# A four-layer graph network on one core: attention of layer 2 in 32-column groups, row sums on GpSimd and ScalarE, layer 0 with its values stationary

## The chip, the cores and the metric

The kernel runs on one core of a Trainium2 chip. The metric is device time in microseconds, the median over runs: 3777.71 us of three runs (3777.58 to 3783.42) for the kernel before.

A core has five engines, each working through its own queue in order. TensorE (PE) multiplies matrices and writes to PSUM, a memory of eight banks of 128 x 512 fp32. VectorE (DVE) and ScalarE (ACT) do elementwise work and read PSUM as well as SBUF, the working memory of 128 partitions; ScalarE also evaluates functions such as exp and ln. GpSimd (POOL) does elementwise work in SBUF. SyncE (SP) issues most DMAs. They wait for each other by semaphores.

## What is computed

32 graphs of 512 nodes with 256 features pass through four layers, each followed by a sum with its input and a layernorm. The layers 0, 1 and 3 are graph attention whose weights come from one value per row and one per column; layer 2 is a transformer block with eight heads of 32 and a mask.

```python
# layer 0: 4 heads of 64; node_adj is 0 or 1 here
h = jnp.einsum('bnd,hde->bhne', nodes_embed, W)
weight = mask * (e_src[:, :, t, :, None] + e_dst[:, :, t, None, :])
weight = jnp.where(node_adj[:, None] == 0, NEG, leaky_relu(weight, 0.01))
dst = jnp.einsum('bhij,bhje->bhie', softmax(weight, axis=-1), h) + bias
out = relu(dst) + h                      # then a layernorm over each head's 64
...
# layer 2: 8 heads of 32
scores = jnp.einsum('bhqd,bhkd->bhqk', q * scale, k)
scores = jnp.where(allowed[:, None], scores, -jnp.inf)   # adj or its transpose or the diagonal
ctx = jnp.einsum('bhqk,bhkd->bhqd', jax.nn.softmax(scores, axis=-1), v)
attn_out = ctx @ Wo.T + bo
x = layernorm(x + attn_out); ff = relu(x @ W1.T + b1) @ W2.T + b2
```

All data are fp32.

## The kernel before

A graph's 512 nodes are four blocks of 128 (R = 4), its 256 features two (K = 2). `graph(b)` is a generator that records one graph's work in small units; each `yield` hands back a place, a number from the table `PLACES` plus `PERIOD` times the graph's number. `heapq.merge` runs the units of all 32 graphs in the order of their places, so that stages of three or four graphs lie beside each other. TensorE's instructions stand in exactly this order (`manual_schedule`); those of the other engines are put in order by a scheduler when the program is built. TensorE works through its queue without overtaking, so a product whose input is late holds everything behind it.

Buffers come from pools. A tile of a tag takes one of its `bufs` buffers and waits until the earlier tile there is no longer used. Each stage has its set ("a": masks and layers 0 and 1; "b": Q/K/V, attention, projection; "c": feed forward, layer 3). PSUM is split alike: `bank` gives two banks to "a", four to "b", two to "c". `part` gives 512-column SBUF tiles: 7, 6 and 5. Every TensorE instruction of the profile has the line L106, since the helper `product` records them all, so they are told apart by the names of their tiles.

Layer 0 (`layer0`): `project` gives h and one source and one destination value per head. The softmax needs no row maximum: with f(s + d) split into exponentials, a row's weights are max(exp(-0.99 s), exp(0.99 d)) times the edge, up to a factor of the row. `along` transposes a head's source values into a row that is equal on all partitions (`gp` in PSUM, `gb` in SBUF); `kept` (L399, VectorE) makes the four weight tiles `pt` of a head (keys on partitions, 512 queries along the row). Then `pt` is the stationary operand, 128 queries at a time, and the values `hv` of the head stream through, 64 columns and a 65th that gives the row's sum: four query blocks by four key blocks, 16 products a head. A reciprocal (L434) and a product (L435) on VectorE end the head in the row layout of `y`. Layer 1 (`o1`) and layer 3 (`o3`) do the same with 257 columns in `attend`.

Layer 2: `qkv` makes Q and K transposed, splits each into a high and a low part and spreads them by 64 KB DMAs on SyncE into the tiles `qk` (three buffers of a pair of heads), so that one product of 128 rows gives an fp32 score. `attention` goes through pairs of heads: four score units (a pair of 512-column scores `s`, exp on ScalarE L559, product with the mask on VectorE L562 or, in the last block, a further product with `shut` on TensorE), then eight products `cp` with V as the stationary operand: 64 columns per head, of which 32 are values and the 33rd is a column of ones that gives the sums. The two heads lie in columns 0 to 63 and 64 to 127 of the array. ScalarE copies `cp` to `cs` (L578). `attended` turns `cs` back into rows (16 transposes `ctp`), divides there (L593, L597), transposes again (8 more `ctp`) and multiplies with Wo (`wop`, L618). Feed forward is 16 units of eight records (`f1p`, relu L644, `f2p`).

Of the kernel before, what the change touches and what calls it, by code (L numbers as in the profile page):

```python
# [26 lines left out]
PERIOD = 12054  # L27
PLACES = {
    "edges": [-2144, -1150, -1132, 1169],
    "x": [2625],  # L30
    "mask": [15570, 16616, 16754, 17543],
    "layer 0": [
        279, 2912, 3852, 3852, 4592, 5702, 5702, 5712, 5965, 5965, 6558, 6558, 6558, 6558,
        6558, 7681, 7681, 7681, 8072, 8072, 8418, 8418, 8418, 8521,
    ],
    "layer 1": [10979, 10979, 11459, 11543, 11663, 11665, 11925, 13128, 13554, 14195, 14884],
    "qkv": [16746, 17776, 18212, 18212, 18212, 18900, 18900, 19096, 20269, 21288],
    "attention": [
        12293, 21738, 21738, 22018, 22018, 22292, 22292, 22687, 22687, 23019, 23479, 23677,
        23718, 23726, 23726, 23726, 25094, 25250, 25378, 25960,  # L40
    ],
    "projection": [26272, 26272, 26332, 26382, 27451, 27561, 28792, 29200, 29412, 29811],
    "feed forward": [
        30548, 31062, 31829, 32245, 32245, 32541, 32692, 33753, 33965, 34306, 34732, 34800,
        35052, 35117, 35751, 36541, 37158, 37317,
    ],
    "layer 3": [39718, 39718, 40714, 40734, 40817, 41334, 41569, 42319, 42319, 42339, 42339],
# [3 lines left out]

# [22 lines left out]
def fast_path(ctx: ExitStack, tc: tile.TileContext, a: dict, out: bass.AP, bad: bass.AP):  # L74
# [21 lines left out]
    VC = DH + 1  # L96
    ND = R * (H + 2 + H2)
    NL = 6
    NV = R * (NL + H)
# [13 lines left out]
    def paced(b, name, units):  # L113

        i = 0
        while True:
            stage[0] = STAGES.get(name, "b")
            try:
                next(units)
            except StopIteration as end:  # L120
                return end.value
            yield PERIOD * b + PLACES[name][i]
            i += 1
# [18 lines left out]
    v = const.tile([P, R, H2 * VC + 2 * DH - VC], F32, name="v")  # L142
    nc.gpsimd.memset(v, 1.0)
# [110 lines left out]
    def bank(name, dtype=F32):  # L254
        shape = [P, 2048 // (2 if dtype == BF16 else 4)]
        n = 4 if stage[0] == "b" else 2
        return ps.tile(shape, dtype, tag="mm" + stage[0], name=name, bufs=n)

    def part(name):

        return buf([P, N], "part", name, {"a": 7, "b": 6, "c": 5}[stage[0]])
# [80 lines left out]
    def along(cols, name):  # L342
# [7 lines left out]
        g = buf([P, N], "gb", name, {"a": 2}.get(stage[0], 1))  # L350
# [52 lines left out]
    def layer0(x, xt, at, rd, mv, var):  # L403
# [12 lines left out]
        nc.vector.tensor_mul(values, values, hv[:, :, :, HO:].to_broadcast([P, R, H, HO]))  # L416
        y = sb.tile([P, R, D], F32, tag="y", name="y0", bufs=3)
        for hh in range(H):
            gb = yield from along(ex[:, 0, hh, :].unsqueeze(2), "gb0")
            pt = [kept("pt0", gb, at[:, j, :], ex[:, 1, hh, j : j + 1]) for j in range(R)]  # L420
            p = bank("o0")
            o = p[:, : R * HC].rearrange("p (r c) -> p r c", r=R)
            for r in range(R):
                yield
                for j in range(R):
                    product(nc.tensor.matmul,
                    o[:, r, :],
                        pt[j][:, r * P : (r + 1) * P],
                        hv[:, j, hh, :],
                        start=j == 0,  # L430
                        stop=j == R - 1,
                    )
            rdh = rd[:, hh * R : (hh + 1) * R].unsqueeze(2)
            nc.vector.reciprocal(rdh, o[:, :, HO:])  # L434
            nc.vector.scalar_tensor_tensor(  # L435
                y[:, :, hh * HO : (hh + 1) * HO],
                o[:, :, :HO],
                0.0,
                rdh.to_broadcast([P, R, HO]),
                op0=ALU.max,  # L440
                op1=ALU.mult,
            )
# [48 lines left out]
    def qkv(x):  # L491
        xt = yield from transposed([x[:, r, :] for r in range(R)], "xt2")
        qk = []
        for c in range(K):
            t = [sb.tile([P, 2, 2, N], F32R, tag="qk", name="qk", bufs=3) for _ in range(2)]
            for s in range(2):
# [18 lines left out]
                for hh in range(4):  # L515
                    for g in range(4):
                        src = (hi, lo)[(g >> s) & 1]
                        nc.sync.dma_start(
                            t[hh // 2][g * DH : (g + 1) * DH, s, hh % 2, :].bitcast(F32),
                            src[hh * DH : (hh + 1) * DH].bitcast(F32),  # L520
                        )
            qk += t
        for r in range(R):
            yield
            p = bank("vp")
            for k in range(K):
# [7 lines left out]
            nc.scalar.copy(  # L534
                v[:, r, : H2 * VC].rearrange("p (h e) -> p h e", h=H2)[:, :, :DH],
                p[:, :D].rearrange("p (h e) -> p h e", h=H2),
            )
# [3 lines left out]
    def attention(qk, a2, shut):  # L541
        cs = []
        for hp in range(H2 // 2):
            pr = []
            for j in range(R):
                yield
                t = sb.tile([P, 2, N], F32, tag="pr", name="pr", bufs=4)
                for i in range(2):
                    s = bank("s")
                    product(nc.tensor.matmul,  # L550
                    s,
                        qk[hp][:, 1, i, j * P : (j + 1) * P],
                        qk[hp][:, 0, i, :],
                        start=True,
                        stop=j < R - 1,
                    )
                    if j == R - 1:
                        product(nc.tensor.matmul, s, identb, shut, start=False, stop=True)
                    nc.scalar.activation(t[:, i, :], s, AF.Exp, scale=QSCALE)  # L559
                if j < R - 1:  # L560
                    edges = a2[:, j, :].unsqueeze(1).to_broadcast([P, 2, N])
                    nc.vector.tensor_mul(t, t, edges)  # L562
                pr.append(t)

            yield
            cp = bank("cp")
            for j in range(R):
                for i in range(2):
                    first = (2 * hp + i) * VC
                    product(nc.tensor.matmul,  # L570
                    cp[i * 2 * DH : (i + 1) * 2 * DH, :],
                        v[:, j, first : first + 2 * DH],
                        pr[j][:, i, :],
                        start=j == 0,
                        stop=j == R - 1,
                    )
            t = part("cs")
            nc.scalar.copy(t, cp)  # L578
            cs.append(t)
        return cs  # L580

    def attended(x, cs, rd):
        ctx_ = []
        for r in range(R):
            yield
            p = bank("ctp")
            for hp in range(H2 // 2):
                product(nc.tensor.transpose,
                    p[:, hp * P : (hp + 1) * P], cs[hp][:, r * P : (r + 1) * P], ident
                )  # L590
            o = p.rearrange("p (h e) -> p h e", h=H2)
            rdr = rd[:, r * H2 : (r + 1) * H2].unsqueeze(2)
            nc.vector.reciprocal(rdr, o[:, :, DH : DH + 1])  # L593
            if r % 2 == 0:
                t = part("ctx").rearrange("p (r d) -> p r d", d=D)
            ctx_.append(t[:, r % 2, :])
            nc.vector.tensor_mul(  # L597
# [816 lines left out]
```

## Time and profile before

| | |
|---|---|
| median of three runs | 3777.71 us |
| the profiled execution: its own time | 3783.98 us |
| the profiled execution: span | 3782.1 us |
| TensorE busy | 3695.1 us |
| VectorE busy | 2659.2 us |
| ScalarE busy | 2034.2 us |
| GpSimd busy | 6.2 us |
| granted TensorE clock, mean | 0.982 |

The span goes from the first to the last instruction of one profiled execution; all durations below come from it. "Busy" is the time in which an engine has at least one instruction in work. The costliest groups of instructions by tile (columns: line, engine, operation, output<-input, shapes, count | busy us, mean ns of one | idle us just before them and what ended it):

```profile
L559 ACT ACTIVATE pr<-s 128x512 f32<-128x512 f32 x1024 | 557.2, 604 | 171.6 <-PE s L106 171.5
...
L106 PE MATMUL o<-hv,pt 128*128 128x65 f32 x4096 | 510.7, 279 | 10.4 <-DVE pt L399 10.4
L106 PE MATMUL f2p<-wf,ft 128*128 128x256 f32 x2048 | 490.2, 382 | 6.4 <-ACT ft L644 6.3
...
L106 PE MATMUL cp<-pr,v 128*64 128x512 f32 x2048 | 469.8, 600 | 0.0
...
L106 PE MATMUL s<-qk 128*128 128x512 f32 x1024 | 412.0, 493 | 4.8 <-ACT pr L559 4.8
```

The second number of a MATMUL row is a modelled duration with the pipeline's length in it: 16 records of 600 ns do not take 9.6 us. What a row costs on TensorE is read from the start of one row to the start of the next.

### The profile page before, as it was taken

To read this page: it belongs to the slowest core of one execution; us is meant where nothing else is said; L and a number is where in the kernel's file an instruction comes from. 1 tells how busy PE (TensorE), PEld (TensorE's weight loads), DVE (VectorE), ACT (ScalarE), POOL (GpSimd) and SP (SyncE) were. 2 spreads that over 40 slices of the span, in tenths; PEclk is the share of its full clock that TensorE was granted. 3 is DMA by queue.
4 is the path that set the end of the run, shared out by engine and by line. 5 is a ranking of instruction groups with operands and counts; after the bars stand their busy time and mean duration, and the time that the engine had idled before them with its cause. 6 is when DMAs were issued, how large, how long until landed. Compare 5 with 4: busy or idle time off the path is not lost.

```text
span 3782.1 us, 53679 instructions
## 1 busy us (share of the span) xinstructions
PE 3695.1 (98%) x19238; PEld 2832.8 (75%) x19238; DVE 2659.2 (70%) x5434; ACT 2034.2 (54%) x4705; POOL 6.2 (0%) x43
## 2 busy tenths in 40 slices
PE   5899999999999999999999999999999999999996
PEld 4577777777777777777787777777777778777765
DVE  4667776777776677776677677677677678677653
ACT  2445565555556555556555565555565555565552
POOL 0000000000000000000000000000000000000000
PEclk6899999999999999999999999999999999999998
DMA  3322222232222222222222222222222222222220
GB/s 105 83 76 59 70 65 71 73 84 61 70 64 71 76 79 63 70 65 72 73 78 65 69 66 70 73 79 68 73 62 68 73 79 68 72 63 61 56 56 12
DMA packets 180434, 261.23 MB, mean 69 GB/s; under 512 B 36801, under 2 KB 72769, under 8 KB 180161
## 3 DMA queue, kind: packets, MB, share of 16 engines
q1 hardware_dynamic: 180160, 257.71, 24.6%
q8 instruction: 156, 2.56, 0.3%
q14 instruction: 118, 0.96, 0.1%
HBM read 106.57 MB, written 16.78 MB: 33 GB/s over the span
## 4 chain that ended last, share of the span: by engine, by line
PE 95%; DVE 3%; ACT 1%; issue 0%; DMA 0%; SPq 0%; ACTq 0%; DVEq 0%
PE o L106 24%; PE cp L106 12%; PE f2p L106 12%; PE f1p L106 12%; PE s L106 8%; PE qkp L106 6%; PE h1p L106 3%; PE h3p L106 3%; PE vp L106 3%; PE h0p L106 3%; PE wop L106 3%; PE gp L106 2%; PE ctp L106 2%; PE xt1p L106 1%; PE xt3p L106 1%; PE ytp L106 1%
## 5 line engine op out<-in xcount | busy, mean ns | idle before, releaser
L562 DVE TENSOR_TENSOR pr<-pr,a 128x1024 f32<-128x1024 f32 x384 | 462.2, 1217 | 357.2 <-ACT pr L559 357.0
L559 ACT ACTIVATE pr<-s 128x512 f32<-128x512 f32 x1024 | 557.2, 604 | 171.6 <-PE s L106 171.5
L399 DVE SCALAR_TENSOR_TENSOR pt<-gb,ex,at 128x512 f32<-128x512 f32 x768 | 527.0, 745 | 36.8 <-ACT gb L351 36.8
L106 PEld LDWEIGHTS o<-hv,pt 128*128 128x128 f32 x4096 | 510.9, 199 | 23.8 <-DVE pt L399 8.3
L106 PE MATMUL o<-hv,pt 128*128 128x65 f32 x4096 | 510.7, 279 | 10.4 <-DVE pt L399 10.4
L106 PE MATMUL f2p<-wf,ft 128*128 128x256 f32 x2048 | 490.2, 382 | 6.4 <-ACT ft L644 6.3
L106 PE MATMUL o<-h,pt 128*128 128x257 f32 x2048 | 485.4, 384 | 6.5 <-DVE pt L399 6.2
L106 PE MATMUL f1p<-yt,wf 128*128 128x256 f32 x2048 | 487.2, 380 | 0.3 <-DVE yt L308 0.3
L106 PE MATMUL cp<-pr,v 128*64 128x512 f32 x2048 | 469.8, 600 | 0.0
L644 ACT ACTIVATE ft<-f1p,cols 128x256 f32<-128x256 f32 x512 | 217.8, 472 | 468.4 <-PE f1p L106 468.3
L106 PEld LDWEIGHTS o<-h,pt 128*128 128x128 f32 x2048 | 384.5, 191 | 102.7 <-PE cp L106 24.3
L106 PEld LDWEIGHTS f2p<-wf,ft 128*128 128x128 f32 x2048 | 376.2, 190 | 82.9 <-issue 26.0
L106 PEld LDWEIGHTS f1p<-yt,wf 128*128 128x128 f32 x2048 | 383.7, 190 | 55.6 <-DVE yt L308 0.7
L106 PE MATMUL s<-qk 128*128 128x512 f32 x1024 | 412.0, 493 | 4.8 <-ACT pr L559 4.8
L282 ACT ACTIVATE y<-y,rs 128x256 f32<-128x256 f32 x768 | 398.3, 591 | 28.4 <-DVE rs L278 28.4
L106 PEld LDWEIGHTS cp<-pr,v 128*64 128x64 f32 x2048 | 135.8, 137 | 257.1 <-issue 159.6
L275 DVE BATCH_NORM_STATS2 bn<-y 128x6 f32<-128x256 f32 x768 | 293.7, 410 | 3.7
L434 DVE RECIPROCAL rd<-o 128x4 f32<-128x4 f32 x128 | 23.3, 182 | 341.6 <-PE o L106 341.6
L106 PEld LDWEIGHTS s<-qk 128*128 128x128 f32 x1024 | 192.9, 191 | 59.9 <-issue 26.8
L106 PE MATMUL qkp<-xt,wqkv 128*128 128x512 f32 x512 | 231.3, 594 | 0.1
L351 ACT COPY gb<-gp 128x512 f32<-128x512 f32 x192 | 112.9, 588 | 151.9 <-PE gp L106 151.9
L578 ACT COPY cs<-cp 128x512 f32<-128x512 f32 x128 | 75.0, 586 | 188.0 <-PE cp L106 187.8
(137 smaller groups left out, 4498.5 us busy)
## 6 DMA issues: line engine op xcount, KB each, us to landing
qk<-hi SPq DMA_DIRECT2D x1024, 64.0 KB, 2.0
qk<-lo SPq DMA_DIRECT2D x1024, 64.0 KB, 2.0
adjt<-in_adjt SPq DMA_DIRECT2D x64, 512.0 KB, 3.9
adj<-in_adj SPq DMA_DIRECT2D x64, 512.0 KB, 3.2
xt<-in_xt SPq DMA_DIRECT2D x32, 512.0 KB, 3.3
x<-in_x SPq DMA_DIRECT2D x32, 512.0 KB, 4.8
out<-y SPq DMA_DIRECT2D x32, 512.0 KB, 3.1
wf<-in_w1t SPq DMA_DIRECT2D x1, 1024.0 KB, 8.6
```

The lines of the kernel that those rows point to most:

```text
L106: latest[0] = what(*args, **kwargs).ins.name
L275: nc.vector.bn_stats(st[:, r, :], y[:, r, :])
L282: nc.scalar.activation(y[:, r, :], y[:, r, :], AF.Identity, bias=rs[:, 1, r : r + 1], scale=rs[:, 0, r : r + 1],)
L351: nc.scalar.copy(g, p)
L399: nc.vector.scalar_tensor_tensor(t, g, f, edges, op0=ALU.max, op1=ALU.mult)
L434: nc.vector.reciprocal(rdh, o[:, :, HO:])
L559: nc.scalar.activation(t[:, i, :], s, AF.Exp, scale=QSCALE)
L562: nc.vector.tensor_mul(t, t, edges)
L578: nc.scalar.copy(t, cp)
L644: nc.scalar.activation(ft[:, f, :], p[:, f, :], AF.Relu, bias=bf1[:, ff + f : ff + f + 1])
```

## The change

Seven edits:

1. Layer 0: the values `hv` are now the stationary operand and `pt` streams through. All four `gb` rows are made first; then, for each key block j, four `pt` tiles, four products of 64 columns into two banks `o0` (two heads a bank) and four of 32 columns into a bank `den0` (the last of them the sums). The three banks are copied to SBUF (`back`), transposed (12 transposes `backp`), and divided there.
2. Layer 2, `attention`: four heads at a time (c = 0, 1), their two score pairs alternating; after every second key block a burst of 16 `cp` records, with V as 32 columns per head, so that four heads lie side by side in the array. No column of ones.
3. The sums of layer 2: GpSimd adds the `pr` tiles of the four key blocks (`add_to`, six adds of 128 x 1024 for each c); four products with a 32-column tile of ones (`den`) add over partitions and give the sum in all 32 rows of a head; ScalarE copies it, takes Ln and Exp(-x), and VectorE multiplies `ct` with it. The second call of `divide` is the last unit of attention. `cp` is copied straight into `ct`, so that `attended` begins at Wo: its 24 transposes and its divisions are gone.
4. Q/K spreading: the columns of the Q and K weights are paired (`wqkvp`), and one DMA of 128 KB carries two heads.
5. PSUM: one set of eight banks for all stages.
6. SBUF: `part` has 9 tiles in "a" and 6 in "c", and holds `gb` too; `pr` has 7 buffers of 128 x 1024 instead of 4.
7. `PLACES` has new numbers; the period is unchanged.

```diff
-    "attention": [
-        12293, 21738, 21738, 22018, 22018, 22292, 22292, 22687, 22687, 23019, 23479, 23677,
...
+    "attention": [
+        18973, 20977, 22864, 22903, 23000, 23000, 23000, 23000, 23117, 23194, 23655, 24186,
...
-        n = 4 if stage[0] == "b" else 2
-        return ps.tile(shape, dtype, tag="mm" + stage[0], name=name, bufs=n)
+        return ps.tile(shape, dtype, tag="mm", name=name, bufs=8)
 
     def part(name):
-        return buf([P, N], "part", name, {"a": 7, "b": 6, "c": 5}[stage[0]])
+        return buf([P, N], "part", name, {"a": 9, "c": 6}[stage[0]])
...
-        g = buf([P, N], "gb", name, {"a": 2}.get(stage[0], 1))
+        g = part(name)
...
+        gbs = []
+        for hh in range(H):
+            gbs.append((yield from along(ex[:, 0, hh, :].unsqueeze(2), "gb0")))
+        den, *ops = (bank(name) for name in ("den0", "o0", "o0"))
+        for j in range(R):
+            pt = [kept("pt0", gbs[hh], at[:, j, :], ex[:, 1, hh, j : j + 1]) for hh in range(H)]
+            yield
+            for hh in range(H):
+                product(nc.tensor.matmul,
+                    ops[hh // 2][hh % 2 * HO : (hh % 2 + 1) * HO, :],
+                    hv[:, j, hh, :HO],
+                    pt[hh],
...
+            for hh in range(H):
+                product(nc.tensor.matmul,
+                    den[hh * DH : (hh + 1) * DH, :],
+                    hv[:, j, hh, HC - DH :],
+                    pt[hh],
...
+        for i, o in enumerate((den, *ops)):
+            t = part("back")
+            evacuate(i, t, o)
+            back.append(t)
...
+        for i in range(1 + H // 2):
+            yield
+            p = bank("backp")
             for r in range(R):
...
+                product(nc.tensor.transpose,
+                    p[:, r * P : (r + 1) * P], back[i][:, r * P : (r + 1) * P], ident
+                )
...
-                for hh in range(4):
+                for hp in range(2):
                     for g in range(4):
                         src = (hi, lo)[(g >> s) & 1]
                         nc.sync.dma_start(
-                            t[hh // 2][g * DH : (g + 1) * DH, s, hh % 2, :].bitcast(F32),
-                            src[hh * DH : (hh + 1) * DH].bitcast(F32),
+                            t[hp][g * DH : (g + 1) * DH, s].bitcast(F32),
+                            src[hp * 2 * DH : (hp + 1) * 2 * DH].bitcast(F32),
                         )
...
+        def add_halves(pr):
+            for hp in range(2):
+                add_to(pr[0][hp], pr[2][hp])
+
+        def divide(c, sums):
+            den = bank("den")
+            for hh in range(4):
+                product(nc.tensor.matmul,
+                    den[hh * DH : (hh + 1) * DH, :],
+                    ones,
+                    sums[hh // 2][:, hh % 2, :],
...
+            t = buf([P, N], "dens", "dens", 2)
+            nc.scalar.activation(t, den, AF.Copy, accum_out=spread[:, 2 * c : 2 * c + 1])
+            nc.scalar.activation(t, t, AF.Ln)
+            nc.scalar.activation(
+                t, t, AF.Exp, scale=-1.0, accum_out=spread[:, 2 * c + 1 : 2 * c + 2]
+            )
+            nc.vector.tensor_mul(ct[:, c, :], ct[:, c, :], t)
+
+        for c in range(K):
+            cp = bank("cp")
+            last, pr = pr, []
             for j in range(R):
+                pr.append([])
+                for hp in range(2):
+                    yield
+                    if last and (j, hp) == (1, 0):
+                        add_halves(last)
+                    t = sb.tile([P, 2, N], F32, tag="pr", name="pr", bufs=7)
...
+                for jj in (j - 1, j):
+                    for hh in range(4):
+                        product(nc.tensor.matmul,
+                        cp[hh * DH : (hh + 1) * DH, :],
+                            v[:, jj, (4 * c + hh) * DH : (4 * c + hh + 1) * DH],
+                            pr[jj][hh // 2][:, hh % 2, :],
...
+                for hp in range(2):
+                    add_to(pr[j - 1][hp], pr[j][hp])
+                if last and j == 1:
+                    yield
+                    divide(0, last[0])
+            nc.scalar.copy(ct[:, c, :], cp)
+        yield
+        add_halves(pr)
+        yield
+        divide(1, pr[0])
+        return ct
+
+    def add_to(t, u):
+        nc.gpsimd.tensor_add(t, t, u)
```

## The prediction

> **What bounds the kernel now.** I read three views in this order: the page's busy times and chain of waits, the busy times of a stretch of ten graphs, and the TensorE timeline of one graph.
>
> ```profile
> span 3782.1 us, 53679 instructions
> ...
> PE 3695.1 (98%) x19238; PEld 2832.8 (75%) x19238; DVE 2659.2 (70%) x5434; ACT 2034.2 (54%) x4705; POOL 6.2 (0%) x43
> ...
> PE 95%; DVE 3%; ACT 1%; issue 0%; DMA 0%; SPq 0%; ACTq 0%; DVEq 0%
> ```
>
> ```profile
> 1000.00:2131.00 1131.00, 1131.00 (x6002) 872.61 (x6001) 825.46 (x1691) 633.99 (x1472) 1.05 (x10) 1.00 0.25 71
> ```
>
> The second fence is a window of 1131 us (columns: length, then busy time of PE, PEld, DVE, ACT, POOL). TensorE has no gap in it. The timeline gives the period: the transposes `xt1p` of neighbouring graphs start at 1861.66 and 1974.76 us, 113.1 us apart. 32 periods are 3619 us; 163 us of the span are start and end, where one graph alone can't fill TensorE. So a graph costs what TensorE's own queue costs; VectorE needs 825.46 / 10 = 82.5 us of the 113.1, ScalarE 63.4, GpSimd 0.1.
>
> A busy row overlaps the next one, so I take TensorE's prices from start to next start:
>
> ```profile
> 1860.70 1.03 PE L106 MATMUL cp<-pr,v 128*64 128x512 f32 x4
> 1861.66 1.09 PE L106 MATMUL xt1p<-ident,y 128*128 128x128 f32 x8
> ```
>
> ```profile
> 1958.16 3.65 PE L106 MATMUL cp<-pr,v 128*64 128x512 f32 x16
> 1961.75 1.99 PE L106 MATMUL f2p<-wf,ft 128*128 128x256 f32 x8
> ...
> 1974.76 1.09 PE L106 MATMUL xt1p<-ident,y 128*128 128x128 f32 x8
> ...
> 2005.67 1.91 PE L106 MATMUL ctp<-ident,cs 128*128 128x128 f32 x16
> 2007.41 1.06 PE L106 MATMUL h0p<-w,xt 128*128 128x264 f32 x4
> ...
> 2030.60 5.31 PE L106 MATMUL qkp<-xt,wqkv 128*128 128x512 f32 x12
> 2035.75 3.64 PE L106 MATMUL o<-h,pt 128*128 128x257 f32 x16
> 2039.22 0.60 PE L106 MATMUL ytp<-ident,y 128*128 128x128 f32 x4
> 2039.66 3.68 PE L106 MATMUL o<-hv,pt 128*128 128x65 f32 x32
> 2043.18 0.60 PE L106 MATMUL gp<-ident,ex 128*128 128x128 f32 x4
> ```
>
> Twelve `qkp` records take 5.15 us, 0.429 us for 512 columns. (A product of fp32 is two records.) Sixteen `cp` records of the same 512 columns take 3.59 us, not 6.9: each uses 64 output columns, and two run at once. 8 x 0.429 = 3.43; with the slower first record behind the burst I count 0.34 us for entering and leaving this mode, 3.77 a burst. A transpose costs 1.74 / 16 = 0.109. The 32 records of one head of layer 0 take 3.52 us, 0.110 each, although 65 columns would stream in far less: each loads 128 columns of weights.
>
> **What the skill says.** The Trainium skill, "TensorEngine Tiling (Array Packing)", Tiling Modes, has 128x64 as two tiles and 128x32 as four, each running its own loads and matmuls, and a drain at a change of mode. The trace agrees for two (3.59 us) and shows the drain (0.34); it has no four. "SBUF — State Buffer", Who interferes with whom: a VectorE instruction with two SBUF inputs and a GpSimd instruction that reads SBUF share one port, and the later one is blocked for the whole of the earlier. No run here shows it yet. "GPSIMD Engine Reference", Elementwise, gives 4497 ns for an fp32 add of 2048 elements.
>
> **The change, for one graph, on TensorE.**
> - Gone: layer 0's four heads, 4 x 3.52 = 14.1. Gone: four `cp` bursts, 4 x 3.77 = 15.1. Gone: 16 + 8 transposes `ctp`, 2.6. Sum 31.8.
> - Layer 0 new: per block j, eight records for the values (64 columns, two at once: 4 x 0.429 = 1.72), eight for the sums (32 columns, four at once: 0.86), the mode's edges 0.34 and half as much for the change of width: 3.08, four times 12.3.
> - `cp` new: the same 64 records, four at once, in four bursts of 16: 4 x 0.429 + 0.34 = 2.06, together 8.2. `den`: twice 0.86, one right behind a `cp` burst, one alone (0.34): 2.1. `backp`: 12 x 0.109 = 1.3.
> - Net 31.8 - 23.9 = 7.9 us less; a gapless period would be 105.2. Scores, feed forward, layers 1 and 3 and projections keep their counts. Bound of the unknown: if four groups run no faster than two, `cp` gains nothing (+6.9), `den` +1.7 and `den0` +3.4, so 12 us more. I take four at once, because two cost nothing extra.
>
> **VectorE, ScalarE, SyncE.** VectorE loses L434 and L435 (23.3 + 54.3 = 77.6 us over 32 graphs, 2.4), L593 and L597 (2.1), one `ct` copy (0.7), and gains two reciprocals (0.4), two products out of PSUM, one copy and two `ct` products (five of about 0.68, the `y<-f2p` row): 1.4 less, 81 of 105. ScalarE loses four `cs` copies and a `ct` copy (2.9) and gains two `ct` copies, two `back` copies and twice copy, Ln, Exp with two accumulator reads (2.2 each): +3.8, so 67. Both lie beside TensorE; if TensorE's cover went, VectorE would be next. The Q/K spreading becomes 1024 DMAs of 128 KB for 2048 of 64 KB (2.0 us to landing). The fourth Q/K tile now waits for both head pairs' walk through all keys, since pairs alternate. From its release to its first use TensorE has some 14 us of work (four feed-forward units of 1.7, a `cp` burst, `xt1p`, scores), against 2 us and some issuing; the graph's output and the next loads queue behind it on SyncE, all needed later. I cost it at nothing.
>
> **GpSimd and the waits, which decide.** Twelve adds of 128x1024 per graph are new. The trace has only a write:
>
> ```profile
> L141 POOL MEMSET hv<- 128x1040 f32 x1 | 1.0, 969 | 0.0
> ...
> L399 DVE SCALAR_TENSOR_TENSOR pt<-gb,ex,at 128x512 f32<-128x512 f32 x768 | 527.0, 745 | 36.8 <-ACT gb L351 36.8
> ...
> L562 DVE TENSOR_TENSOR pr<-pr,a 128x1024 f32<-128x1024 f32 x384 | 462.2, 1217 | 357.2 <-ACT pr L559 357.0
> ```
>
> An add can't take less than that write, 1.0 us; the skill's figure gives an estimate of 2.25; with each add waiting for a VectorE instruction to finish (1.2) and stretching, 3.4. I take 2.25: 27 us of GpSimd per graph. Of VectorE's work some two thirds have two SBUF inputs (24 `pt` x 0.69, 12 `pr` x 1.2 and 15 of 1024 elements x 1.2 are 49 us, with smaller ones 54). If two thirds of the adds' time block VectorE, it needs 81 + 18 = 99 of 105: it fits, but nothing is left for lateness. Three places then stop TensorE, whose queue runs in order:
> - First block of layer 0: three of its four `pt` tiles take buffers that layer 1's `pt` hold until the attend directly ahead of it ends. Three times 0.69 us beside the block's own start: 1.0.
> - The second `den`: four adds lie between the last `cp` burst and it (9.0, starting 0.6 before the burst ends), against two attends (3.5), one block of layer 0 (3.1) and `xt3p` (0.9) on TensorE. Short by 0.9; half a VectorE instruction before each add makes it 3.3; 1.0 is already spent at the stop above: 2.3. Behind it wait layer 0 and everything later.
> - `xt1p`: in the first half of attention VectorE has eleven products of 1.2, two reductions of 0.7 and statistics of 2.3, together 17; with two adds in the way 21.5, and four normalising rows of ScalarE (L282, 0.59 each) 23.9. TensorE gets there after 16 scores and four `shut` (0.23 each by the timeline, 4.6), eight feed-forward units (13.8), two bursts (4.1) and two more scores: 22.9. Late by 1.0.
> Together 4.3: 105.2 + 4.3 = 109.5.
>
> PSUM in one set of eight: layer 0 holds three banks, `cp` and the feed-forward sum one each. Six scores follow each other once with five banks free, and ScalarE frees one each 0.6 us (L559): a few tenths, inside the 4.3. Its other sign is also possible, since stages may borrow each other's banks; TensorE waits for no bank today, so I count no gain.
>
> The sum: 32 x 109.5 + 163 = 3667 us against the profile's 3782.1. Its own run was 3784.0, the median is 3777.7, 4.4 under the span: 3663 us.
>
> **Rivals.**
> - No contention and no stop: 105.2 x 32 + 163 = 3529, less 4: 3525. For it: TensorE has no gap at all now with VectorE at 73%. Against: the second `den` is late even on unblocked adds.
> - Slower, by the shared port. Place: attention, where ten of the twelve adds meet `pr` and the 1.2 us products. Price: adds of 3.4 us, 41 us per graph, nine tenths of it blocking VectorE: 81 + 37 = 118, less 2 that records of neighbours overlap: 116. It decides once stops exceed 7.9 us, that is when blocking passes some 32 us per graph. 32 x 116 + 163 = 3875, less 4: 3871. For it: the adds stand in the chain that frees the seven `pr` buffers. Against: VectorE's idle quarter.
> - Slower, since the array takes four groups two at a time: 105.2 + 12 = 117.2, then the adds are covered: 3913, less 4: 3909. Speaks for it that the trace shows two only; against, that two run at exactly half.
> - Gain and stops cancel: about 3778.
>
> **How the numbers follow.** The measurement can tell a difference of 0.2%, 7.6 us. Forecast (108 to 112.7 per period, 3615 to 3765) 0.49; no stop 0.15; cancelled 0.05; port 0.23; two at a time 0.08. Faster 0.64, same 0.05, slower 0.31. The likeliest case's own range is 3615 to 3765. For eight in ten I go from 3520, which takes in the no-stop case, to 3860, the cheaper half of the port case.
>
> **What would show it.** `cp` bursts of 16 records at 2.1 us from start to next start: four at once; 3.8 proves me wrong. Layer 0's blocks near 3.1 us. `den` on TensorE waiting for POOL, `o0` for `pt`, `xt1p` for ScalarE, each a microsecond or two per graph. VectorE's `pr` rows longer than 1217 ns: the shared port. POOL adds near 2.25 us; over 3 us would turn the sign.

## The result, and the profile after

The changed kernel takes 4166.88 us (median of four runs, 4163.49 to 4167.96) against 3780.57 us for the kernel before, measured beside it. The ratio is 1.1019, with a 95% interval of 1.0999 to 1.1038: a tenth slower, where 3663 us and a gain were forecast.

The page of the changed kernel: span, busy times, and the chain of waits by engine. Its profiled execution took 4166.27 us.

```profile
span 4164.5 us, 49491 instructions
...
PE 3734.5 (90%) x17254; PEld 2420.2 (58%) x17318; DVE 3146.7 (76%) x5114; ACT 2102.6 (50%) x4993; POOL 1082.2 (26%) x427
...
PE 53%; DVE 31%; issue 9%; ACT 6%; DMA 0%; SPq 0%; DVEq 0%; ACTq 0%
```

TensorE was 98% busy and carried 95% of the chain. Now it is 90% busy, and VectorE carries 31% of the chain although it is idle a quarter of the time. So no engine has become the bound: TensorE waits, at places, for a VectorE that is late at those places. The mean granted clock fell too, from 0.982 to 0.938.

The costliest groups by tile (after the bar: busy us, mean ns of one | idle us just before them, and what ended it):

```profile
L641 POOL TENSOR_TENSOR pr<-pr 128x1024 f32<-128x1024 f32 x384 | 1077.0, 2831 | 2450.5 <-PE cp L104 2281.3
L397 DVE SCALAR_TENSOR_TENSOR pt<-gb,ex,at 128x512 f32<-128x512 f32 x768 | 691.2, 950 | 148.4 <-ACT gb L349 79.3
L614 DVE TENSOR_TENSOR pr<-pr,a 128x1024 f32<-128x1024 f32 x384 | 484.7, 1278 | 408.3 <-ACT pr L611 408.2
L611 ACT ACTIVATE pr<-s 128x512 f32<-128x512 f32 x1024 | 536.6, 609 | 36.1 <-PE s L104 36.1
L104 PE MATMUL f2p<-wf,ft 128*128 128x256 f32 x2048 | 540.0, 411 | 7.8 <-ACT ft L684 7.7
L104 PE MATMUL o<-pt,hv 128*64 128x512 f32 x1024 | 398.1, 696 | 148.9 <-DVE pt L397 89.4
...
L104 PE MATMUL cp<-pr,v 128*32 128x512 f32 x2048 | 295.7, 604 | 53.2 <-DVE pr L614 53.1
...
L276 DVE SCALAR_TENSOR_TENSOR rs<-mvs,rs 128x4 f32<-128x4 f32 x192 | 157.4, 820 | 45.1 <-ACT rs L266 44.2
L104 PE MATMUL xt1p<-ident,y 128*128 128x128 f32 x256 | 84.0, 434 | 117.9 <-ACT y L280 116.4
```

`cp` got what it was to get: busy 295.7 us instead of 469.8. But three products now have idle time in front of them that was not there: `o` of layer 0 148.9, `xt1p` 117.9, `cp` 53.2 us. And VectorE's rows have grown: `pt` from 745 to 950 ns. The row to stop at is L276. It handles 128 x 4 elements and takes 820 ns on average.

The starts of `xt1p` are 126.3 us apart (113.1 before). A TensorE timeline of one such period shows where (columns: start, us, the instructions, idle time before them and what ended it):

```profile
2021.90 1.05 PE L104 MATMUL cp<-pr,v 128*32 128x512 f32 x4 [0.30 <-DVE pr L614]
2024.17 1.91 PE L104 MATMUL cp<-pr,v 128*32 128x512 f32 x12 [1.22 <-DVE pr L614]
...
2033.62 2.81 PE L104 MATMUL xt1p<-ident,y 128*128 128x128 f32 x8 [3.43 <-ACT y L280]
2036.22 3.62 PE L104 MATMUL f2p<-wf,ft 128*128 128x256 f32 x8
...
2071.20 1.92 PE L104 MATMUL cp<-pr,v 128*32 128x512 f32 x16
2073.05 3.74 PE L104 MATMUL o<-h,pt 128*128 128x257 f32 x16
2078.81 1.07 PE L104 MATMUL o<-pt,hv 128*64 128x512 f32 x2 [2.02 <-DVE hv L414]
2081.57 1.97 PE L104 MATMUL o<-pt,hv 128*64 128x512 f32 x2 [1.69 <-DVE pt L397]
2084.41 2.54 PE L104 MATMUL o<-pt,hv 128*64 128x512 f32 x4 [0.88 <-DVE pt L397]
```

Two clusters of stops: 4.95 us at `cp` and `xt1p`, 4.59 us at layer 0's first key block. Behind each, work takes longer than it should: eight `f2p` records take 3.62 us instead of about 1.9, two of `o` 1.97 instead of 1.07. The windows of those moments (columns: length, PE, PEld, DVE, ACT, POOL busy, then the granted clock, DMA share, GB/s) say why:

```profile
2033.60:2036.20 2.60, 2.52 (x8) 1.64 (x9) 0.94 (x4) 2.60 (x7) 1.63 (x1) 0.50 0.00 0
2036.20:2039.60 3.40, 3.40 (x10) 2.72 (x9) 1.82 (x2) 2.04 (x5) 0.00 (x0) 0.50 0.29 19
...
2081.50:2084.40 2.90, 1.97 (x2) 0.30 (x3) 2.90 (x3) 0.00 (x0) 2.22 (x1) 0.50 0.00 0
2084.40:2088.50 4.10, 4.09 (x13) 0.77 (x13) 2.20 (x6) 0.47 (x1) 0.00 (x0) 0.54 0.30 41
```

Behind each cluster the granted clock is about half (0.50 to 0.54) for six to seven us.

VectorE and GpSimd in the same two stretches show what VectorE was late with. GpSimd first, then VectorE:

```profile
2013.95 5.67 POOL L641 TENSOR_TENSOR pr<-pr 128x1024 f32<-128x1024 f32 x2 [56.52 <-PE cp L104]
2023.10 12.13 POOL L641 TENSOR_TENSOR pr<-pr 128x1024 f32<-128x1024 f32 x4 [3.47 <-DVE y L473]
...
2051.31 4.70 POOL L641 TENSOR_TENSOR pr<-pr 128x1024 f32<-128x1024 f32 x2 [0.26 <-PE cp L104]
2072.40 11.32 POOL L641 TENSOR_TENSOR pr<-pr 128x1024 f32<-128x1024 f32 x4 [16.39 <-PE cp L104]
```

```profile
2014.46 2.95 DVE L302 TENSOR_TENSOR y<-y,st 128x1024 f32<-128x1024 f32 x1 [0.40 <-ACT st L266]
2017.45 3.26 DVE L472 TENSOR_TENSOR y<-y,gam_b 128x1024 f32<-128x1024 f32 x1
...
2025.57 1.86 DVE L645 TENSOR_TENSOR y<-y,bo_b 128x1024 f32<-128x1024 f32 x1
...
2027.46 3.26 DVE L646 TENSOR_TENSOR y<-y,ln2b_b 128x1024 f32<-128x1024 f32 x1
2030.64 2.29 DVE L276 SCALAR_TENSOR_TENSOR rs<-mvs,rs 128x4 f32<-128x4 f32 x1
```

Each of these five has two inputs in SBUF and stands beside an add of GpSimd. With the adds moved to VectorE (first experiment) the four large ones take 1.2 us and L276 0.16 us. Together the five take 13.6 instead of 5.0 us: 8.6 us lost in one stretch of VectorE's queue. L302, L472 and L276 belong to the layernorms that `xt1p` needs; L645 and L646 belong to `attended` and merely stand in the queue ahead of L276. L276 is the end of a layernorm's statistics; ScalarE's rows L280 wait for it, `xt1p` for these, and all of TensorE behind `xt1p`. At layer 0 the same happens: `pt`, L276 and `pt` again stand against the four adds from 2072.40 on.

### The profile page after: what moved, and what is told of

Same layout as the page of the kernel before. It is cut to its first block, busy times and chain, and to the rows that moved or that the text cites. A ratio compares the mean times of both kernels' runs of the same rounds, so it can differ in the third digit from the quotient of the medians.

```text
span 4164.5 us, 49491 instructions
## 1 busy us (share of the span) xinstructions
PE 3734.5 (90%) x17254; PEld 2420.2 (58%) x17318; DVE 3146.7 (76%) x5114; ACT 2102.6 (50%) x4993; POOL 1082.2 (26%) x427
## 3 DMA queue, kind: packets, MB, share of 16 engines
q8 instruction: 140, 2.29, 0.2%
## 4 chain that ended last, share of the span: by engine, by line
PE 53%; DVE 31%; issue 9%; ACT 6%; DMA 0%; SPq 0%; DVEq 0%; ACTq 0%
PE o L104 12%; PE f2p L104 7%; DVE pt L397 6%; PE qkp L104 5%; PE f1p L104 5%; PE den L104 4%; PE s L104 4%; DVE rs L276 3%; DVE bn L273 3%; PE h1p L104 3%; PE h3p L104 3%; DVE pr L614 3%; PE wop L104 3%; ACT y L280 2%; DVE y L302 2%
## 5 line engine op out<-in xcount | busy, mean ns | idle before, releaser
L641 POOL TENSOR_TENSOR pr<-pr 128x1024 f32<-128x1024 f32 x384 | 1077.0, 2831 | 2450.5 <-PE cp L104 2281.3
L397 DVE SCALAR_TENSOR_TENSOR pt<-gb,ex,at 128x512 f32<-128x512 f32 x768 | 691.2, 950 | 148.4 <-ACT gb L349 79.3
L611 ACT ACTIVATE pr<-s 128x512 f32<-128x512 f32 x1024 | 536.6, 609 | 36.1 <-PE s L104 36.1
L104 PE MATMUL f2p<-wf,ft 128*128 128x256 f32 x2048 | 540.0, 411 | 7.8 <-ACT ft L684 7.7
L104 PE MATMUL o<-pt,hv 128*64 128x512 f32 x1024 | 398.1, 696 | 148.9 <-DVE pt L397 89.4
L280 ACT ACTIVATE y<-y,rs 128x256 f32<-128x256 f32 x768 | 398.0, 590 | 259.7 <-DVE rs L276 259.7
L104 PE MATMUL s<-qk 128*128 128x512 f32 x1024 | 354.0, 462 | 10.8 <-DMA qk<-lo 7.5
L104 PE MATMUL cp<-pr,v 128*32 128x512 f32 x2048 | 295.7, 604 | 53.2 <-DVE pr L614 53.1
L104 PEld LDWEIGHTS o<-pt,hv 128*64 128x64 f32 x1024 | 84.9, 149 | 394.7 <-DVE pt L397 183.7
L265 ACT ACTIVATE rs<-mvs,eps1e-05_70 128x4 f32<-128x4 f32 x192 | 57.1, 298 | 496.5 <-DVE mvs L274 494.5
L276 DVE SCALAR_TENSOR_TENSOR rs<-mvs,rs 128x4 f32<-128x4 f32 x192 | 157.4, 820 | 45.1 <-ACT rs L266 44.2
L104 PE MATMUL xt1p<-ident,y 128*128 128x128 f32 x256 | 84.0, 434 | 117.9 <-ACT y L280 116.4
```

The lines of the kernel that those rows point to most:

```text
L104: latest[0] = what(*args, **kwargs).ins.name
L265: nc.scalar.activation(out, variance, AF.Ln, bias=eps[e])
L276: nc.vector.scalar_tensor_tensor(rs[:, 1, :], mv[:, :, 0], -1.0, rs[:, 0, :], op0=ALU.mult, op1=ALU.mult)
L280: nc.scalar.activation(y[:, r, :], y[:, r, :], AF.Identity, bias=rs[:, 1, r : r + 1], scale=rs[:, 0, r : r + 1],)
L397: nc.vector.scalar_tensor_tensor(t, g, f, edges, op0=ALU.max, op1=ALU.mult)
L641: nc.gpsimd.tensor_add(t, t, u)
```

## The experiments

The theory: VectorE and GpSimd share a way to read SBUF, and the blocked instructions, one after another in the same chain, stop TensorE, whose clock then falls. The rivals: the new order itself is to blame (places, PSUM in one set, buffers); or the sums come late to `den`. Experiments 1 to 6 are single runs, the others medians of four or seven.

**1. All sums on VectorE.** Nothing else moves.

```diff
-        nc.gpsimd.tensor_add(t, t, u)
+        nc.vector.tensor_add(t, t, u)
```

> The twelve adds of a graph go to VectorE instead of GpSimd. Port theory (GpSimd's reads block VectorE's two-input instructions, and the late results stop TensorE): pr, pt and the 1024-element products are back at 1.22 and 0.75 us, VectorE gets 12 x 1.2 = 14 us more work, 95 of some 110; period 107 to 113 us, 3590 to 3780 us in all. Order theory (the new order and the shared buffers make the stops, whoever adds): VectorE has more to do in the same order, so the stops at xt1p and o0 stay or grow; 4150 us or more.

3758.91 us (before, beside it: 3777.13). That is 408 us less than the changed kernel, although VectorE has the adds to do as well (459.1 us in all, 14.3 a graph). Its rows:

```profile
L397 DVE SCALAR_TENSOR_TENSOR pt<-gb,ex,at 128x512 f32<-128x512 f32 x768 | 535.4, 746 | 87.9 <-ACT gb L349 78.1
...
L641 DVE TENSOR_TENSOR pr<-pr 128x1024 f32<-128x1024 f32 x384 | 459.1, 1212 | 107.2 <-PE cp L104 107.0
...
L276 DVE SCALAR_TENSOR_TENSOR rs<-mvs,rs 128x4 f32<-128x4 f32 x192 | 30.7, 160 | 41.2 <-ACT rs L266 41.2
```

All are back at the durations that they had before the change. TensorE's order, the places and PSUM in one set are those of the changed kernel, so by themselves they don't cost the 386 us. Only one stop of more than a microsecond is left in a period, at the second `den`, whose four adds are now behind other work of VectorE. It lasts 3.71 us and the clock behind it is 0.53:

```profile
1997.71 3.03 PE L104 MATMUL den<-pr,ones 128*32 128x512 f32 x8 [3.71 <-DVE mvs L274]
```

**2. All sums on TensorE.** `den` accumulates over all four key blocks in the bursts; no add anywhere.

```diff
-                for hp in range(2):
-                    add_to(pr[j - 1][hp], pr[j][hp])
...
+                for jj in (j - 1, j):
+                    for hh in range(4):
+                        product(nc.tensor.matmul,
+                        den[hh * DH : (hh + 1) * DH, :],
+                            ones,
+                            pr[jj][hh // 2][:, hh % 2, :],
+                            start=jj == 0,
+                            stop=jj == R - 1,
+                        )
```

> No adds: TensorE sums over all four key blocks itself with 48 more den records per graph, 12 steps of 0.43 us = 5.2 us. Port theory: GpSimd idle, VectorE at its old durations and 81 us, period 104.5 + 5.2 and a few tenths = 110 to 112, so 3680 to 3750 us. Order theory: the stops at xt1p and o0 stay, and 5 us come on top: 4200 to 4350 us.

3866.39 us, period 116.3: the direction of the theory, its size missed. The `den` records cost 1.83 us in each of four bursts, 5.4 us more than the two `den` of the change. And with the adds gone, the `o` of layer 0's second key block take 5.0 us where 1.9 would do. They wait for `pt`: VectorE, which has no gap there, makes these four tiles between other work, the next graph's mask among it. The eighth experiment comes back to this.

**3. The same tiles, written instead of added.** Three memsets take the place of each add, so that GpSimd is about as busy and everyone waits for it as before, but it reads nothing. This kernel leaves out the sums.

```diff
-        nc.gpsimd.tensor_add(t, t, u)
+        for x in (t, u, t):
+            nc.gpsimd.memset(x, 1.0)
```

> Leaves out the sums: each add becomes three writes of GpSimd to the same two tiles, 3 x 0.97 = 2.9 us, as long as an add (2.83) and behind the same waits, but reading nothing from SBUF. Port theory: VectorE's rows return to 1.22 and 0.75 us and most of the stops are gone, period 106 to 109 us, 3550 to 3650 us. Chain theory (the time that GpSimd holds the pr tiles and the sums is what makes TensorE wait): about 4165 us, as now. Where both have a share, between.

3606.9 us, period 107.6. GpSimd is busy for 32.3 us a graph (33.9 in the changed kernel), and VectorE isn't blocked:

```profile
L642 POOL MEMSET pr<- 128x1024 f32 x1152 | 1029.8, 956 | 2065.9 <-PE cp L104 2065.8
...
L276 DVE SCALAR_TENSOR_TENSOR rs<-mvs,rs 128x4 f32<-128x4 f32 x192 | 30.7, 160 | 44.6 <-ACT rs L266 43.8
```

This excludes the rival that TensorE stops because GpSimd's part takes long: it takes as long here. Writing alone doesn't block VectorE; what counts is that the adds read. It also is the picture of the change without its cost. Three rows of its timeline:

```profile
2036.93 1.94 PE L104 MATMUL o<-pt,hv 128*64 128x512 f32 x8
2038.80 1.06 PE L104 MATMUL den<-pt,hv 128*32 128x512 f32 x8
2039.79 3.70 PE L104 MATMUL qkp<-xt,wqkv 128*128 128x512 f32 x8
```

One block of layer 0 takes 2.86 us from start to next start.

**4. Products in the gaps.** The changed kernel, with seven products that nobody reads before `xt1p` and twelve before layer 0's first block.

```diff
+    def warm(n):
+        p = bank("warm")
+        for _ in range(n):
+            product(nc.tensor.matmul,
+                p[:, :D], ident, w0[:, 0, :D], start=True, stop=True)
...
+            if name == "xt1" and k == 0:
+                warm(7)
...
+            if j == 0:
+                warm(12)
```

> After with 14 further TensorE records of 256 columns (3.0 us) before xt1p and 24 (5.2 us) before the first block of layer 0, into a bank that nothing reads; they lie in the stops. Clock theory [...]: granted clock back near 0.98, period down by 3 to 5 us, 4010 to 4070 us. If the lower clock costs nothing, since the engine waits anyway: 4160 us or more.

4064.98 us at a clock of 0.985, and the adds as long as in the changed kernel (2833 ns). The period falls from 126.3 to 122.2 us. TensorE has to wait as long as before: the third of layer 0's `pt` lets it go on 11.4 us after the start of the attend ahead of it, in both kernels. So about 102 us of the 386 are the halved clock behind the stops, not the stops.

**5. The adds in the kernel before.** Twelve GpSimd adds a graph, on a tile that nobody else touches, in the kernel before the change.

```diff
             nc.scalar.copy(t, cp)
             cs.append(t)
+            for i in range(3):
+                in_place(nc.gpsimd.tensor_add(extra, extra, extra))
...
```

> The kernel before, with 12 GpSimd adds of 128 x 1024 a graph, three behind each cp burst, on a tile that nothing else reads or writes, so that nobody waits for them; the output is unchanged. If the shared way to SBUF costs the same in any order, as much as between the kernel with the sums on VectorE and the one with them on GpSimd (408 us): 4100 to 4250 us. If the cost comes from how little slack the new order leaves between VectorE's chains and TensorE, and the old order has more, then clearly less: 3800 to 3980 us. If the adds cost only their result's lateness and not the port: 3775 to 3800 us.

3993.96 us, 210 more than the kernel before beside it (3783.71): between the two expectations, a little above the lower one. Nobody waits for these adds, so their lateness costs nothing, and their length shows in VectorE's rows (1217 ns before):

```profile
L583 POOL TENSOR_TENSOR extra<-extra 128x1024 f32<-128x1024 f32 x384 | 877.0, 2284 | 2807.2 <-PE cp L106 2787.1
...
L564 DVE TENSOR_TENSOR pr<-pr,a 128x1024 f32<-128x1024 f32 x384 | 576.4, 1521 | 301.5 <-ACT pr L561 298.6
```

Over ten periods VectorE has 93.4 us a graph here (82.5 before), 10.9 blocked, and the period grows by 6.4 us. In the changed kernel VectorE has 98.6 us (82.3 with the memsets), 16.3 blocked, and the period is 18.7 us longer. A blocked microsecond costs 0.6 us in the old order and 1.15 us in the new one. Part of the difference is the clock, 0.99 here and 0.95 in the changed kernel over these periods. My reading of the rest is that the adds of the new order stand opposite chains for which TensorE waits; no run varies this alone.

**6. A third of the adds on GpSimd.** First level on VectorE, second level (four adds a graph) on GpSimd.

```diff
-                add_to(pr[0][hp], pr[2][hp])
+                nc.gpsimd.tensor_add(pr[0][hp], pr[0][hp], pr[2][hp])
...
-        nc.gpsimd.tensor_add(t, t, u)
+        nc.vector.tensor_add(t, t, u)
```

> Of the 12 adds a graph the 8 of the first level are on VectorE, the 4 of the second level on GpSimd: a third of the dose. If the loss is proportional to the adds on GpSimd (408 us for 384 adds, 1.06 us each), 128 x 1.06 = 136 us over the kernel with all adds on VectorE: about 3895 us. If it comes from blocked instruction following blocked instruction, it grows faster than the dose: under 3830 us. If the second den, which waits for the last two adds, is what costs: above 3900 us, with a stop over 6 us at that den.

3879.08 us, 120 more than with all sums on VectorE, near the 136 of proportion. My guess of a steeper course fell. It isn't a clean dose, though: the stop at `den` is gone and layer 0's `o` waits for `pt` instead (142.8 us in all), so two changes are in this number.

**7. Moving the last stop (four runs).** With the sums on VectorE, I tried to put the second `den` where its adds are done. First only its place is changed. In the trace it then stands in the middle of layer 3's `h3p`, eight records before it and eight behind:

```diff
-        24186, 24186, 25013, 25013, 25013, 25057, 25057, 25997, 26361, 27661, 29010, 30393,
+        24186, 24186, 25013, 25013, 25013, 25057, 25057, 25997, 26361, 27661, 29900, 30393,
```

> As with all adds on VectorE (3758.9 us), with the second den alone moved behind layer 3's projection (place 29900 instead of 29010). If the stop of 3.7 us before that den is what is left over against TensorE's own work, about 4.5 us a graph go with it (the stop and the low clock behind it): 3600 to 3640 us. If the late VectorE chain merely stops the next product (o of layer 0, h3p or xt2p), 3700 to 3760 us.

3842.2 us, slower than both expectations and than the kernel before (ratio 1.0162, 1.0145 to 1.0179). The stop moved to layer 0's second key block and grew:

```profile
2035.92 1.10 PE L104 MATMUL xt3p<-ident,y 128*128 128x128 f32 x8
2042.57 4.34 PE L104 MATMUL o<-pt,hv 128*64 128x512 f32 x8 [5.55 <-DVE pt L397]
```

The wait at `den` had covered this one. Then the same place, with the second level of the sums left to TensorE (`den` over two tiles, eight records more a time), which takes four adds off VectorE:

```diff
-            for hh in range(4):
...
-                    start=True,
-                    stop=True,
...
+            for jj in (0, 2):
+                for hh in range(4):
...
+                        start=jj == 0,
+                        stop=jj == 2,
...
-        add_halves(pr)
```

> VectorE makes the first-level sums (8 adds of 128 x 1024 a graph), the second level is left to TensorE, which accumulates den over two sums (8 den records a time instead of 4); the first den stands before the fourth score pair of c = 1, the second one behind layer 3's projection h3p (place 29900 instead of 29010). No add is on GpSimd. Port theory with the stops: the period of 112.6 us (sums all on VectorE) loses the stop of 3.7 us at the second den and about 1 us of low clock behind it and pays 2 x 0.5 us for the further den records: about 108 to 109 us, 3610 to 3650 us in all, faster than both kernels. If TensorE's further den records cost as in the run where all four blocks were summed there (1.8 us for 16 records, so 0.9 for 8), or if the den now waits for VectorE at its new places, 3680 to 3760.

3809.91 us (ratio 1.0078, 1.0062 to 1.0095): the stop at the second block is 3.14 us. The clock behind it isn't low in every graph: over its first three us it is 1.00 in 8 of the 26 graphs between 500 and 3400 us and 0.50 to 0.65 in the other 18. And with that block, and those after it, moved behind `h3p` as well (the second `den` is put a little later, too):

```diff
-        -12543, -12543, -12543, -12543, -327, -327, -327, -327, 3670, 5361, 6479, 6924,
+        -12543, -12543, -12543, -12543, -327, -327, -327, -327, 3670, 6292, 6580, 7500,
```

> As the first level on VectorE and the second on TensorE (3809.9 us), with new places for layer 0: its second key block, whose four pt tiles VectorE can make only when the first block has freed their buffers, no longer follows one transpose after the first block but behind xt3p and layer 3's whole projection; the third and fourth block and the second den are moved behind it in the same way. If the stop at the second block (3.1 us and about 1.3 us of low clock behind it, every graph) is what keeps that kernel above the one with all sums on VectorE, about 4.4 us a graph go: 3650 to 3690 us. If h3p, which now follows xt3p at once, waits for the copies of xt3p from PSUM instead, 1 to 2 us of it come back: 3690 to 3740 us. If the third or fourth block now waits for its own pt, 3740 or more.

3951.59 us (1.0451, 1.0433 to 1.0468). `h3p` now waits for VectorE's copy of `xt3p`, which stands behind the same work:

```profile
2096.18 4.13 PE L104 MATMUL h3p<-w3g,xt 128*128 128x258 f32 x10 [4.87 <-DVE xt L306]
```

With `den` put between `xt3p` and `h3p`:

> As the run before it, with the second den put between xt3p and h3p, so that it covers the copies of xt3p. If the two sums that it reads are done by then (two adds on VectorE instead of four stand before it): 3630 to 3680 us, below the run before it. If it waits for VectorE as in the kernel with all sums on VectorE (3.7 us there): 3720 to 3780 us.

3899.31 us (1.0315, 1.0298 to 1.0333): `den` doesn't wait, but `h3p` still does, 3.48 us. In the first and the third of these runs I had named the product that then waited, and underrated it.

**8. VectorE's work in that stretch.** Between layer 0's first and second block VectorE also had 1.6 us of mask work for the next graph. I moved it behind the second block, in the kernel with the second level on TensorE; and then also left the last two adds of the first level to TensorE.

```diff
-    "mask": [13037, 13222, 15804, 17801],
+    "mask": [13037, 17450, 17460, 18700],
```

> As the first level on VectorE and the second on TensorE with the second den behind h3p (3809.9 us), with VectorE's mask work for the next graph (1.6 us that stood between the first and the second key block of layer 0) placed behind the second block. If VectorE's work in that stretch, and not the buffers, sets the second block's stop of 3.1 us: it falls to about 1.5 us, and the low clock behind it becomes shorter, 3700 to 3770 us. If the four pt buffers that come free with the first block set it, no change: 3790 to 3815 us.

3768.1 us (0.9971, 0.9959 to 0.9982), faster than the kernel before and the changed kernel, if only by 0.3% against the former. The waits at the second block are down to 0.38 us. The cause named there was right: VectorE's work in that stretch, not the buffers. None of the runs of this and the next experiment, nor of the seventh, comes below the plain move of the first (3758.91 us, one run).

> As the run before it, and the two adds of c = 1's last two key blocks (2.4 us on VectorE just before those pt tiles) are left to TensorE, whose second den then accumulates over three tiles (8 more records of den, 0.9 us). VectorE's work as the cause: the stop at the second block falls below 0.7 us and the clock stays up, 3640 to 3710 us, faster than both kernels. If another wait takes its place (xt3p's copies, the third block, cp for the mask product): 3710 to 3780 us.

3768.09 us (0.9967, 0.9956 to 0.9979), no gain by the second step: the 24 `den` records now take 2.71 us, and the period stays at 112.7.

```profile
2006.50 2.78 PE L104 MATMUL den<-pr,ones 128*32 128x512 f32 x24
2009.21 2.01 PE L104 MATMUL h3p<-w3g,xt 128*128 128x258 f32 x8
```

**9. The same with all sums on VectorE.** Mask work, second-level adds and `den` later; in the second run all four last adds behind the second block.

> All sums on VectorE (3758.9 us), with VectorE's mask work and the two second-level adds of c = 1 placed behind layer 0's second key block and the second den behind h3p. If that kernel is above its gapless work only because VectorE has more to do between the first and the second key block than TensorE has, the stop of 3.7 us and the low clock behind it go and the den stays at four products: a period of about 110 us, 3670 to 3710 us. If VectorE, 95 us of 112.6 here, is too full for any order of this kind, the stop reappears at another product (den, xt2p, qkp): 3750 to 3840 us.

> As the run before it, with all four adds of c = 1's last sums behind the second key block, so that nothing of the sums stands before its pt tiles, and the den behind the third block. If the order on VectorE in that stretch is what is left: 10 to 40 us below the run before it, 3640 to 3690 us. If the four adds together now make the third block, xt2p or wop wait: above the run before it.

3792.43 us (1.0026, 1.0014 to 1.0037) and 3823.99 us (1.0117, 1.0101 to 1.0134): stops of 1.35 and 1.27 us at the second block and of 1.34 and 1.82 us at `qkp` remain, all ended by VectorE (`pt`, and the copy of `xt2p`). So these two further orders did not mend it. VectorE has 95.2 us a graph with all sums (ten periods of the first experiment); whether an order exists in which that is hidden stays open.

## Why the prediction was wrong

- **The work was right.** `cp`, 2.06 a burst: 1.98 on average with the memsets. A block of layer 0, 3.08: 2.86 where it has no wait. `den`, 2.1 for two: 1.97. `backp`, 1.3: 1.3. The gapless 105.2 us stands against 107.6 with the memsets, of which 0.9 are two visible waits. Four column groups at once: right; the rival with two at a time is out.
- **The amount of blocking came out near, by luck.** 18 us forecast, 16.3 measured; VectorE 99 forecast, 98.6 measured. But the forecast was two thirds of 27 us of adds, and the trace has about half of 33.9: two errors that offset each other.
- **An add** was put at 2.25 us. The pair at 2051.31, with VectorE idle beside most of it, takes 2.35 each; the mean in the changed kernel is 2.83, and those that meet VectorE's two-input instructions take up to 3.40. (The 2.28 of the fifth experiment is no second measure of it: those adds read one tile twice.) 2.83 is inside the bounds of 1.0 to 3.4, and under the 3 us that were said to turn the sign. The sign turned all the same.
- **The failed step is the sum of stops, 4.3 us.** TensorE is idle for 10.5 us a graph instead (126.3 less 115.8 busy), and its rows take 9.1 us longer than with the memsets (115.8 against 106.7). "It fits, but nothing is left for lateness" was true, and then the lateness was priced too low, in two terms. At `xt1p` I let two adds stand in VectorE's way, 4.5 us, and came to a lateness of 1.0. Six adds ran beside that stretch, and they blocked five instructions for 8.6 us. The prediction's own sum with 8.6 for 4.5 is late by 5.1, and the trace has 4.95 (0.30 and 1.22 at `cp`, 3.43 at `xt1p`). At layer 0's first block I counted three `pt` of 0.69 and put the four adds that run then only against the second `den`. They block `pt`, L276 and three more `pt`: 4.59 instead of 1.0.
- **The second `den`**, 2.3 forecast: no wait in the changed kernel. The stop at layer 0 comes before it, and the adds are done at 2083.72, ahead of `den` at 2089.52. With the sums on VectorE it is 3.71.
- **No price for the clock.** The Trainium skill, "TensorE: Matmul & The Clock Gate", Why this matters for your kernels, warns of idle gaps over about 3 us between matmul bursts. I counted no loss after a stop, a term put at nothing without a reason. The trace agrees with the page at `xt1p`, 0.50 behind 3.43 us. It goes beyond it at layer 0, where the clock is 0.50 behind 2.02 and 1.69 us with one 1.07 us row between them, and it shows no sharp line: behind the 3.14 us of the seventh experiment the clock fell in some graphs only. The fourth experiment prices the low clock at 102 us, 3.2 a graph.
- **The rival by the port** had the right mechanism and the wrong way: it wanted 41 us of adds and nine tenths of them blocking, so that VectorE becomes the bound, and it put the turn of the sign at some 32 us of blocking. 16.3 us were enough, and VectorE never was the bound. The Trainium skill, "SBUF — State Buffer", Who interferes with whom, says that only a GpSimd instruction that reads SBUF contends with two-input VectorE instructions. The memsets bear this out (L276 at 160 ns under the same GpSimd load).
- **DMAs and PSUM at nothing**: right. In the changed kernel the scores wait 7.5 us in all for the DMAs of `qk`, although these, twice as large, take 3.7 to 3.9 us to land instead of 2.0, and 1.5 us for ScalarE's exp (L611), which frees their banks.

## What to carry to other kernels

In this kernel a second engine that shares a resource with a busy one could not be priced by the time that it blocks on average; it mattered which instructions it met. Follow the chain that feeds the in-order engine, with everything that stands ahead of it in the same queue, and count a delay for every member that runs beside a blocking instruction, small ones too (here 0.7 to 2.1 us each, beside adds of 2.83). And before a wait is moved, look for the wait that it has been covering: here two moves brought out a longer one than they removed (5.55 for 3.71 us, 4.87 for 3.14).

## What was unexpected

- A VectorE instruction of 128 x 4 elements, 0.16 us by itself, took 2.29 us beside an add of GpSimd: its size doesn't protect it.
- A wait of 3.43 us was followed by about 6 us at half the clock. `xt1p` and the `f2p` behind it took 2.60 and 3.42 us from start to start. With the gap filled (fourth experiment) they took 2.08 and 1.72, so the clock cost 2.2 us there; with the memsets, where `xt1p` doesn't wait for ScalarE either, 0.87 and 1.73.
- 32-column `den` records of 512 columns: 0.98 us for eight, 1.85 for sixteen, 2.71 for 24. Every further eight cost nearly as much as the first, so a sum over more tiles on TensorE is paid for in full.
